# Four pairs of PSUM banks for large and small tiles, adjacent keys in the window attention, spread bias products and a new weighting in the planner

## The chip, the cores and the metric

The kernel runs on one core of one Trainium2 chip. The core has a TensorE (PE in the profile; PEld is its loading of the stationary operand), a VectorE (DVE), a ScalarE (ACT), a GpSimd (POOL) and a SyncE (SP), which here only issues DMAs. The engines run side by side, each through its own queue in order, and wait for each other through semaphores. Matrix products land in PSUM, from where DVE or ACT take them into SBUF. The metric is the device time of one execution in microseconds (us). The three runs of the kernel before took 1317.29, 1317.72 and 1319.53 us, so the median is 1317.72 us.

## The reference, cut to what matters

The input is `x` of shape (4, 512, 128), float32. Six stages follow, each added to `x`:

```
x = x + 0.5 * rwkv_ffn(layernorm(x))          # three 128x128 products, relu^2, sigmoid
x = x + attention(layernorm(x))               # 16 heads of 64, 512 keys, relative bias
x = x + 0.5 * rwkv_ffn(layernorm(x))
x = x + 0.5 * local(layernorm(x))             # two layers
x = x + min_gru(layernorm(x))                 # a scan over time
x = x + 0.5 * local(layernorm(x))             # two layers
```

One layer of `local` is what the change touches most. With 8 heads of 64 and a window of 64:

```
h = shift_token(x)
q, k, v = split(h @ wqkv)                     # then l2norm, scales and rotary factors on q and k
bk, bv  = the window before and the own window of k and v      # 128 keys for each 64 queries
sim  = q @ bk.T, masked to  i - 64 <= j <= i
x    = x + softmax(sim) @ bv @ wo
h    = layernorm(shift_token(x)) * lg + lb
a, g = split(h @ w1 + b1)                     # 341 columns each
x    = x + (a * gelu(g)) @ w2 + b2
```

## The kernel before, in words

Everything is kept in SBUF, with the 128 features on the partitions and 512 times of one sequence along a row (`xTs[b]`). There are four sequences b; a sequence has NT = 4 blocks t of 128 times.

**A planner orders the work.** The kernel's code doesn't issue instructions. A `Recorder` for each engine writes operations down with a cost in us, a virtual due time `vt` and the tiles that they touch; `plan.bundle(cost, mode)` makes one operation of several PE products. `Plan.plan` then simulates the engines and picks at each step the operation that can start first, the one with the least due time among those that can start together. It looks `HORIZON` us of due time ahead. A PE bundle whose `mode` (full, row or col) differs from the last one's is counted `MODE_BIAS` later, an ACT function that needs another table `TABLE_BIAS` later. `Plan.emit` issues what was picked, engine by engine in that order, and `pin` fixes it. So the order within an engine, and the buffers, are decided by this plan before the kernel runs, and the chip waits where the real durations differ. `STEP`, `TURN`, `ATTN`, `LATE` (lines 49 and 50) set the due times: a query block of the attention is due every `STEP`, a step of a local layer every `TURN`.

**Modes.** In `full` mode a product uses the whole 128x128 array. `row` mode takes halves of the contraction (64 rows each, two heads at once): the scores of the attention (64*128, one bundle is two products of 512 columns) and of the window attention (64*64). `col` mode takes halves of the output columns: the weighted sums over the values (128*64).

**Buffers.** `Memory` (lines 344 to 399) gives tiles out by kind. In SBUF 33 buffers serve either one `pair` tile or two `half` tiles each. In PSUM there are two tiles of kind A (`psA`, two banks each, 1024 columns) and four of kind S (`psS`, one bank each, 512 columns).

**Attention** (`unit`, lines 545 to 627). For each of 8 pairs of heads and 4 sequences, four query blocks q: a bundle of scores into an A tile; two DVE operations that add the bias and find the maximum (`tensor_tensor_reduce`, line 587); two exponentials on ACT; a multiplication on POOL; later eight transposes into two S tiles, copied out by DVE (j = 0) and ACT (j = 1); after two q, a col bundle `po` (line 616).

**Local layer** (`local_layer`, lines 637 to 830). Nine kinds of work run as a pipeline over t, listed in `order` and `behind` (lines 792 to 794): `rotate`, `values`, `turn`, `soften`, `turn_back`, `weigh`, `turn_outputs`, `project`. `turn` transposes q and k into `qTs[t]` and `kTs[t]`, two halves. `soften` makes the scores of the two 64-query windows of block t. For the lower window (PSUM partitions 0 to 63) the own 64 keys are in `kTs[t]`, the 64 before them in `kTs[t - 1]` (zeros at t = 0), so there are two products of 64 columns for each head; for the upper window one of 128 columns. That is 24 products in a bundle, 64 such bundles. `turn_back` puts the values of the lower window together in `vm` by two DMAs, own keys on partitions 0 to 63 and earlier ones on 64 to 127.

**Bias products** (lines 945 to 957). `lb @ w1` of each layer, six products of one column in one S tile for each layer (12 in all), each followed by a DVE addition out of the same tile. All are due near the end of the attention.

Of the kernel before, what the change touches and what calls it, by code (L numbers as in the profile page):

```python
# [9 lines left out]
ALU = mybir.AluOpType  # L10
# [4 lines left out]
P = 128  # L15
B, T, D = 4, 512, 128
NT = T // P
# [28 lines left out]


PAIRS = 33
STEP, TURN = 3.6, 11.7
ATTN, LATE, LAG = 25.0, 410.0, 4  # L50

class Tile:

# [61 lines left out]
class Plan:  # L115
# [1 line left out]

    LATENCY, HORIZON, SWITCH, TABLE = 0.07, 36.0, 0.1, 1.28  # L120
    MODE_BIAS, TABLE_BIAS = 2.0, 11.3

    def __init__(self, tc, memory):
        self.tc, self.nc, self.memory = tc, tc.nc, memory
# [45 lines left out]
    def plan(self):  # L170
# [13 lines left out]
        free, mode, order, wire = {}, "full", [], 0.0  # L184
        unplanned = sorted(self.ops, key=lambda o: -o.vt)
        table = None
        while unplanned:
            while unplanned and unplanned[-1].start is not None:
                unplanned.pop()
# [76 lines left out]
    def emit(self, order):  # L266
        table = None
        for op in order:
            since = len(self.nc.cur_bb.bb.instructions)
            if op.table and op.table != table:  # L270
                table = op.table
                self.nc.scalar.add_instruction(  # L272
                    mybir.InstLoadActFuncSet(
                        name=self.nc.get_next_instruction_name(),
                        engine=mybir.EngineType.Activation, act_func_set_id=table,
                    )
                )
            for call in op.calls:
                call()
            self.pin(since)  # L280
# [63 lines left out]
class Memory:  # L344


    def __init__(self, slots, pairs):
        self.slots = slots
        self.pairs = pairs
        self.free = {k: [0.0] * len(s) for k, s in slots.items()}  # L350
        self.halves = [[0.0, 0.0] for _ in pairs]

    def when(self, kind):
        inf = float("inf")
        if kind == "half":
            return min((f for h in self.halves for f in h if f is not None), default=inf)
        if kind == "pair":
            return min((max(h) for h in self.halves if None not in h), default=inf)
        return min((f for f in self.free[kind] if f is not None), default=inf)

    def take(self, t):
        if t.kind == "half":
            at = [
                (f, h[1 - j] is not None, i, j)
                for i, h in enumerate(self.halves) for j, f in enumerate(h) if f is not None
            ]
            first = min(a[0] for a in at)
            _, _, i, j = min((a for a in at if a[0] <= max(first, self.now)), key=lambda a: a[1:])
            self.halves[i][j], t.slot, base = None, (i, j), self.pairs[i][:, j * HALF : (j + 1) * HALF]
        elif t.kind == "pair":  # L370
            at = [(max(h), -i) for i, h in enumerate(self.halves) if None not in h]
            first = min(a[0] for a in at)
            i = -min((a for a in at if a[0] <= max(first, self.now)), key=lambda a: a[1])[1]
            self.halves[i], t.slot, base = [None, None], (i, None), self.pairs[i]
        else:
# [3 lines left out]
        if t.kind == "va":  # L379
            t.real = base  # L380
            return
        n = 1
        for d in t.shape[1:]:
            n *= d
        v = base[: t.shape[0], :n]
        if len(t.shape) > 2:
            names = "abc"[: len(t.shape) - 1]
            v = v.rearrange(
                f"p ({' '.join(names)}) -> p {' '.join(names)}", **dict(zip(names, t.shape[1:]))
            )  # L390
        t.real = v

    def give(self, t):
        if t.kind == "half":
            self.halves[t.slot[0]][t.slot[1]] = t.end
        elif t.kind == "pair":
            self.halves[t.slot[0]] = [t.end, t.end]
        else:
            self.free[t.kind][t.slot] = t.end


HALF = T + 8
# [3 lines left out]
def tile_macaron(ctx: ExitStack, tc: tile.TileContext, i: dict, out: bass.AP):  # L406
# [6 lines left out]
    def real(name, shape, pool=pool):  # L413
# [36 lines left out]
    pool_.memset(tiny[:, 1:2], 1e-24)  # L450
    ones_sb = const("ones", [P, P])
    pool_.memset(ones_sb, 1.0 / D)
    zeros_sb = const("zeros", [P, WIN])
    pool_.memset(zeros_sb, 0.0)

    def vec(col, n=P):
        return vecs[:n, col : col + 1]
# [179 lines left out]
    def local_layer(l, h):  # L637
# [47 lines left out]
        def turn(t):  # L685

            u = us.pop(t)
            qTs[t] = plan.tile("half", [P, H1 // 2, P])
            kTs[t] = plan.tile("half", [P, H1 // 2, P])
            for g, dst in enumerate((qTs[t], kTs[t])):  # L690
                ptp = plan.tile("S", [P, H1 // 2, P])
                with plan.bundle(0.44):
                    for pr in range(H1 // 2):
                        c = g * INNER + pr * P
                        pe.transpose(ptp[:, pr, :], u[:, c : c + P], ident)
                act.copy(dst, ptp)

        def soften(t):


            qT, kT = qTs.pop(t), kTs[t]
# [26 lines left out]
        def turn_back(t):  # L728


            vm = vms[t] = plan.tile("half", [P, H1, DX])
            dma.dma_start(out=vm[0:64], in_=vas[t][0:64])
            if t == 0:
                pool_.memset(vm[64:128], 0.0)
# [189 lines left out]
    for l in range(DEPTH):  # L924
# [17 lines left out]
            pool_.tensor_tensor(tab[l], tab[l], sc, ALU.mult)  # L942
            tab[l] = tab[l].rearrange("p n (g d) -> p n g d", d=DH)

        pb = plan.tile("S", [P, 2, NHC])
        for g in range(2):
            for c in range(NHC):
                n = min(P, HID - c * P)
                c0 = g * HID + c * P
                pe.matmul(  # L950
                    pb[:n, g, c : c + 1], lhsT=w1_sb[l][:, c0 : c0 + n], rhs=vec(V_LNB + l),
                    start=True, stop=True,
                )
                v0 = (V_B1G if g else V_B1A) + l * NHC + c
                dve.tensor_tensor(
                    b1_sb[:n, l, g, c : c + 1], pb[:n, g, c : c + 1], vec(v0, n), ALU.add
                )
# [21 lines left out]
def _constants():  # L979
# [12 lines left out]


    p, c = np.arange(P)[:, None], np.arange(KEYS)[None, :]
    upper = p < WIN
    at = np.where(upper, (c + WIN) % KEYS, c)
    seen = (at >= p % WIN) & (at <= p % WIN + WIN)
    mask = np.stack([seen & ~(upper & (at < WIN)), seen], axis=1)
    mask = np.where(mask, f4(0.0), f4(NEG)).astype(f4)

    half = np.arange(0, DH, 2, dtype=f4)
# [73 lines left out]
```

## Time and profile before

| what | value |
| --- | --- |
| runs of the kernel before | 1317.29, 1317.72, 1319.53 us (median 1317.72) |
| the profiled execution, its own time | 1317.3 us |
| its span in the trace, first to last instruction | 1315.5 us |
| granted TensorE clock, mean over the span | 0.992 |
| DVE, ACT, POOL busy | 970.1, 893.1, 741.4 us |
| PE products in the trace | 10892 |
| ACT table loads, each 1283 ns | 76 |

The span is 1.8 us shorter than the profiled execution's time: what lies around it is outside the trace. The work runs through the stages one after another with some overlap at their borders. Up to about 50 us come the loads and the first `rwkv`, to about 480 us the attention, to about 600 us the second `rwkv` and the first steps of the local layers, to about 880 us the first local stage, to about 1000 us the recurrence and the passage into the second local stage, and from there on the second local stage.

A float32 product that is no transpose appears as two records in the trace (6614 products make 10892 records, 2336 of them transposes with one record each). Records of PE overlap, and their ends are modelled. What a bundle costs PE is therefore read as the distance from its start to the start of the next bundle.

### The profile page before, as it was taken

The numbers are of one execution on the slowest core, as the hardware profiler recorded it, in microseconds if no ns is written. First come the engines' busy times: TensorE is split into PE (matmuls) and PEld (weight loads), VectorE is DVE, ScalarE is ACT, GpSimd is POOL, SyncE is SP. The second block draws the span as 40 slices with busy tenths as digits, with TensorE's granted clock in tenths as the row PEclk, the third lists the DMA queues.
The fourth block names the chain that finished last, engine by engine and source line by source line (L and its number), as shares of the span: only waits on it lengthen the run. The fifth ranks groups of instructions, "written<-read, shape, count | busy, mean of one in ns | idle before, by whom it ended". The sixth has DMA issues, their size and how long they took to land. (4 is left out here: it accounts for less than half of the span.)

```text
span 1315.5 us, 27611 instructions
## 1 busy us (share of the span) xinstructions
PE 1265.9 (96%) x10892; PEld 791.5 (60%) x10892; DVE 970.1 (74%) x1875; ACT 893.1 (68%) x1698; POOL 741.4 (56%) x445
## 2 busy tenths in 40 slices
PE   7999999999999999899999999999889999999997
PEld 3455566556565655457766666664355766666673
DVE  4766666667677657888887787876888887787774
ACT  5866666656666646767777767777577777777774
POOL 3645455554554736768856655623578766665620
PEclk9999999999999989999999999999899999999999
DMA  4775000000000000010101100000110101100000
GB/s 114 224 223 175 0 1 1 1 1 1 1 2 0 1 0 17 13 26 22 31 22 22 26 22 22 22 1 1 29 26 22 30 17 27 26 22 22 14 18 24
DMA packets 26773, 41.79 MB, mean 32 GB/s; under 512 B 3386, under 2 KB 14180, under 8 KB 26644
## 3 DMA queue, kind: packets, MB, share of 16 engines
q1 hardware_dynamic: 26356, 39.95, 11.2%
q8 instruction: 86, 1.41, 0.5%
q14 instruction: 43, 0.35, 0.1%
q10 hardware_dynamic: 288, 0.08, 0.0%
HBM read 23.99 MB, written 9.49 MB: 25 GB/s over the span
## 5 line engine op out<-in xcount | busy, mean ns | idle before, releaser
L302 POOL TENSOR_TENSOR pair<-pair,small 128x1024 f32<-128x1024 f32 x256 | 485.5, 1902 | 319.7 <-DVE small L302 281.0
L302 PEld LDWEIGHTS psS<-ident,pair 128*128 128x128 f32 x2320 | 266.4, 142 | 155.3 <-issue 122.1
L302 POOL TENSOR_TENSOR pair<-pair,pair 128x1024 f32<-128x1024 f32 (+2 forms) x111 | 213.7, 1929 | 218.7 <-DVE pair L302 112.2
L302 ACT COPY pair<-psS 128x512 f32<-128x512 f32 x484 | 264.5, 591 | 86.1 <-PE psS L302 68.4
L302 PE MATMUL psS<-ident,pair 128*128 128x128 f32 x2320 | 310.0, 277 | 11.7 <-DVE pair L302 5.0
L302 PE MATMUL psS<-pair,pair 128*64 128x65 f32 (+3 forms) x2352 | 263.9, 310 | 1.0 <-DVE pair L302 1.0
L302 ACT ACTIVATE pair<-pair,small 128x512 f32<-128x512 f32 x256 | 182.8, 717 | 120.2 <-DVE small L302 119.9
L302 PEld LDWEIGHTS psS<-pair,pair 128*64 128x64 f32 (+1 forms) x2352 | 172.3, 144 | 68.7 <-issue 16.9
L302 DVE CUSTOM_DVE_ANT_0 pair<-psA,pair 128x512 f32<-128x512 f32 x256 | 167.0, 684 | 44.5 <-PE psA L302 44.5
L302 DVE COPY pair<-psS 128x512 f32<-128x512 f32 (+1 forms) x192 | 114.7, 599 | 69.4 <-PE psS L302 61.6
L302 DVE TENSOR_REDUCE small<-pair 128x8 f32<-128x1024 f32 (+1 forms) x128 | 151.8, 1211 | 0.8
L302 PE MATMUL psA<-pair 64*128 64x512 f32 (+3 forms) x728 | 142.7, 513 | 0.6 <-DVE pair L302 0.6
L302 ACT ACTIVATE pair<-pair 128x512 f32<-128x512 f32 (+1 forms) x152 | 122.2, 810 | 30.8 <-DVE pair L302 13.5
L302 PE MATMUL psA<-pair,pair 64*64 64x64 f32 (+2 forms) x2728 | 134.1, 263 | 1.8 <-DVE pair L302 1.8
L302 PE MATMUL psA<-wqkv,pair 128*128 128x512 f32 x256 | 123.7, 606 | 2.8 <-DVE pair L302 2.8
L302 DVE TENSOR_TENSOR pair<-psA,sin 128x512 f32<-128x512 f32 x128 | 87.5, 684 | 39.4 <-ACT pair L302 29.3
L302 ACT ACTIVATE pair<-psA 128x1024 f32<-128x1024 f32 x64 | 65.7, 1026 | 65.3 <-PE psA L302 52.8
L302 PEld LDWEIGHTS psA<-pair,pair 64*64 64x64 f32 (+1 forms) x2728 | 84.9, 135 | 30.7 <-issue 22.8
L272 ACT ACT_TABLE_LOAD x75 | 96.2, 1283 | 1.3
L302 PE MATMUL psA<-pair,w 128*128 128x512 f32 (+1 forms) x192 | 89.3, 598 | 4.1 <-DVE pair L302 2.8
L302 DVE TENSOR_TENSOR pair<-psA,mask 128x1024 f32<-128x1024 f32 x64 | 78.0, 1219 | 11.2 <-PE psA L302 5.6
L302 PEld LDWEIGHTS psA<-pair 64*128 64x128 f32 (+2 forms) x728 | 52.5, 170 | 55.4 <-issue 44.9
(81 smaller groups left out, 1454.1 us busy)
## 6 DMA issues: line engine op xcount, KB each, us to landing
pair<-va SPq DMA_DIRECT2D x112, 130.0 KB, 2.3
table<-tdram SPq DMA_DIRECT2D x16, 511.5 KB, 7.0
pair<-table SPq DMA_DIRECT2D x16, 448.0 KB, 4.0
wqkv<-in_L_ffn_wqkv_dram SPq DMA_DIRECT2D x2, 768.0 KB, 8.1
pair<-in_x_dram SPq DMA_DIRECT2D x4, 256.0 KB, 3.5
out_dram<-pair SPq DMA_DIRECT2D x4, 256.0 KB, 2.3
w<-in_L_ffn_w_dram SPq DMA_DIRECT2D x2, 341.0 KB, 5.9
pair<-in_L_attn_wq_dram SPq DMA_DIRECT2D x8, 64.0 KB, 5.3
```

The source lines that it names most:

```text
L272: self.nc.scalar.add_instruction(mybir.InstLoadActFuncSet(name=self.nc.get_next_instruction_name(), engine=mybir.EngineType.Activation, ac ...
L302: real(*[a.resolve() if isinstance(a, View) else a for a in args], **{k: a.resolve() if isinstance(a, View) else a for k, a in kw.items()},)
```

## The change: what it does

1. **PSUM**: the two A and four S tiles become four pairs of banks, `banks0` to `banks3`. An A tile takes a whole pair, an S tile one bank of a pair; the rule by which they are given out is that of the SBUF pairs and halves.
2. **Adjacent keys**: `kTs[t]` becomes a pair tile of 64 + 128 columns, with the last 64 keys of the block before ahead of its own. A DMA copies those 64 columns out of `kTs[t]` into `kTs[t + 1]`; at t = 0 POOL clears them. `soften` then has, for each head and each window, one product of 128 columns: 16 in a bundle. The mask, and the two halves of `vm`, follow the new order of the keys.
3. **Bias products**: the six of a layer become three bundles of two products, in S tiles of their own and with due times spread over the attention.
4. **Planner**: `MODE_BIAS` from 2.0 to 10.2, `TABLE_BIAS` from 11.3 to 17.0, `HORIZON` from 36.0 to 27.4, `TURN` from 11.7 to 11.1, `ATTN` from 25.0 to 20.5. A PE operation that follows a pause is counted dearer (`IDLE`, `COLD`). The first ACT operation loads table set 6 ahead of itself (`FIRST`); before, the first two ACT operations came with a load each.

```diff
-STEP, TURN = 3.6, 11.7
-ATTN, LATE, LAG = 25.0, 410.0, 4
+STEP, TURN = 3.6, 11.1
+ATTN, LATE, LAG = 20.5, 410.0, 4
...
-    LATENCY, HORIZON, SWITCH, TABLE = 0.07, 36.0, 0.1, 1.28
-    MODE_BIAS, TABLE_BIAS = 2.0, 11.3
+    LATENCY, HORIZON, SWITCH, TABLE = 0.07, 27.4, 0.1, 1.28
+    IDLE, COLD, FIRST = 2.5, 8.0, 6
+    MODE_BIAS, TABLE_BIAS = 10.2, 17.0
...
-            if op.engine == "tensor" and op.mode != mode:
-                cost, mode = cost + self.SWITCH, op.mode
+            if op.engine == "tensor":
+                if op.mode != mode:
+                    cost, mode = cost + self.SWITCH, op.mode
+
+                if at - free.get("tensor", -self.IDLE) >= self.IDLE:
+                    cold = at + self.COLD
+                cost += min(cost, max(0.0, cold - at) / 2)
...
-            if op.table and op.table != table:
-                table = op.table
+            need = op.table or (self.FIRST if op.engine == "scalar" and not op.bytes and table is None else table)
+            if need != table:
+                table = need
                 self.nc.scalar.add_instruction(
...
     memory = Memory(
         {
-            "A": [real(f"psA{n}", [P, 2 * T], psum) for n in range(2)],
-            "S": [real(f"psS{n}", [P, T], psum) for n in range(4)],
...
-        [real(f"pair{n}", [P, 2 * HALF]) for n in range(PAIRS)],
+        {
+            ("half", "pair"): [real(f"pair{n}", [P, 2 * HALF]) for n in range(PAIRS)],
+            ("S", "A"): [real(f"banks{n}", [P, 2 * T], psum) for n in range(4)],
+        },
     )
...
             qTs[t] = plan.tile("half", [P, H1 // 2, P])
-            kTs[t] = plan.tile("half", [P, H1 // 2, P])
-            for g, dst in enumerate((qTs[t], kTs[t])):
+
+            if t == 0:
+                kTs[t] = plan.tile("pair", [P, H1 // 2, WIN + P])
+                pool_.memset(kTs[t][:, :, :WIN], 0.0)
+            for g, dst in enumerate((qTs[t], kTs[t][:, :, WIN:])):
...
+            if t + 1 < NT:
+                kTs[t + 1] = plan.tile("pair", [P, H1 // 2, WIN + P])
+                dma.dma_start(out=kTs[t + 1][:, :, :WIN], in_=kTs[t][:, :, P:])
...
-            with plan.bundle(1.02, "row"):
+            with plan.bundle(0.9, "row"):
                 for pr in range(H1 // 2):
                     for j in range(2):
                         hp = slice(j * DH, (j + 1) * DH)
-                        before = kTs[t - 1][hp, pr, WIN:] if t else zeros_sb[hp, :]
-                        for c, keys in enumerate((kT[hp, pr, :WIN], before)):
+                        for blk in range(2):
+                            c = slice(blk * WIN, (blk + 1) * WIN)
                             pe.matmul(
-                                sc[:WIN, j, pr, c * WIN : (c + 1) * WIN], lhsT=qT[hp, pr, :WIN],
-                                rhs=keys, start=True, stop=True,
+                                sc[c, j, pr, :], lhsT=qT[hp, pr, c],
+                                rhs=kT[hp, pr, blk * WIN : blk * WIN + KEYS], start=True, stop=True,
                             )
-                        pe.matmul(
-                            sc[WIN:, j, pr, :], lhsT=qT[hp, pr, WIN:], rhs=kT[hp, pr, :],
-                            start=True, stop=True,
-                        )
...
-            dma.dma_start(out=vm[0:64], in_=vas[t][0:64])
+            dma.dma_start(out=vm[64:128], in_=vas[t][0:64])
...
-                dma.dma_start(out=vm[64:128], in_=vas[t - 1][64:128])
+                dma.dma_start(out=vm[0:64], in_=vas[t - 1][64:128])
...
-        pb = plan.tile("S", [P, 2, NHC])
-        for g in range(2):
-            for c in range(NHC):
...
+        now = plan.vt
+        for c in range(NHC):
+            n = min(P, HID - c * P)
+            plan.vt = ATTN + (l * NHC + c + 2) * B * NT * STEP
+            pb = plan.tile("S", [P, 2])
+            with plan.bundle(0.3):
+                for g in range(2):
+                    c0 = g * HID + c * P
+                    pe.matmul(
+                        pb[:n, g : g + 1], lhsT=w1_sb[l][:, c0 : c0 + n], rhs=vec(V_LNB + l),
+                        start=True, stop=True,
+                    )
...
+        plan.vt = now
```

More of the change, by code (lines that the diff above doesn't have):

```diff
@@ L183, in plan @@
                 ready.setdefault(op.engine, []).append((0.0, op))
-        free, mode, order, wire = {}, "full", [], 0.0
+        free, mode, order, wire, cold = {}, "full", [], 0.0, 0.0
         unplanned = sorted(self.ops, key=lambda o: -o.vt)
-        table = None
+        table = self.FIRST
         while unplanned:
@@ L344, with __init__ @@
 class Memory:
-    def __init__(self, slots, pairs):
+    def __init__(self, slots, paired):
         self.slots = slots
-        self.pairs = pairs
         self.free = {k: [0.0] * len(s) for k, s in slots.items()}
-        self.halves = [[0.0, 0.0] for _ in pairs]
+        self.paired, self.now = {}, 0.0
+        for (small, large), pairs in paired.items():
+            halves = [[0.0, 0.0] for _ in pairs]
+            self.paired[small] = pairs, halves, False
+            self.paired[large] = pairs, halves, True
     def when(self, kind):
         inf = float("inf")
[L355 to L359, printed above, removed]
-    def take(self, t):
[L362 to L375, printed above, removed]
+        if kind not in self.paired:
+            return min((f for f in self.free[kind] if f is not None), default=inf)
+        _, halves, large = self.paired[kind]
+        if large:
+            return min((max(h) for h in halves if None not in h), default=inf)
+        return min((f for h in halves for f in h if f is not None), default=inf)
+    def take(self, t):
+        if t.kind not in self.paired:
             f = self.free[t.kind]
@@ L378, in take @@
             f[i], t.slot, base = None, i, self.slots[t.kind][i]
-        if t.kind == "va":
-            t.real = base
-            return
+            if list(base.shape) == list(t.shape):
+                t.real = base
+                return
+        else:
+            pairs, halves, large = self.paired[t.kind]
+            if large:
+                at = [(max(h), -i) for i, h in enumerate(halves) if None not in h]
+                first = max(min(at)[0], self.now)
+                i = -min((a for a in at if a[0] <= first), key=lambda a: a[1])[1]
+                halves[i], t.slot, base = [None, None], (i, None), pairs[i]
+            else:
+                at = [
+                    (f, h[1 - j] is not None, i, j)
+                    for i, h in enumerate(halves) for j, f in enumerate(h) if f is not None
+                ]
+                first = max(min(at)[0], self.now)
+                _, _, i, j = min((a for a in at if a[0] <= first), key=lambda a: a[1:])
+                n = pairs[i].shape[1] // 2
+                halves[i][j], t.slot, base = None, (i, j), pairs[i][:, j * n : (j + 1) * n]
         n = 1
@@ L393, in give @@
     def give(self, t):
[L394 to L398, printed above, removed]
+        if t.kind not in self.paired:
             self.free[t.kind][t.slot] = t.end
+            return
+        i, j = t.slot
+        for k in (0, 1) if j is None else (j,):
+            self.paired[t.kind][1][i][k] = t.end
 HALF = T + 8
@@ L452, in tile_macaron @@
     pool_.memset(ones_sb, 1.0 / D)
-    zeros_sb = const("zeros", [P, WIN])
-    pool_.memset(zeros_sb, 0.0)
     def vec(col, n=P):
@@ L695, in turn @@
                         pe.transpose(ptp[:, pr, :], u[:, c : c + P], ident)
-                act.copy(dst, ptp)
+                act.copy(dst, ptp, n=T)
+            if t + 1 < NT:
+                kTs[t + 1] = plan.tile("pair", [P, H1 // 2, WIN + P])
+                dma.dma_start(out=kTs[t + 1][:, :, :WIN], in_=kTs[t][:, :, P:])
         def soften(t):
-            qT, kT = qTs.pop(t), kTs[t]
+            qT, kT = qTs.pop(t), kTs.pop(t)
             sc = plan.tile("A", [P, 2, H1 // 2, KEYS])
-            with plan.bundle(1.02, "row"):
+            with plan.bundle(0.9, "row"):
                 for pr in range(H1 // 2):
@@ L731, in turn_back @@
             vm = vms[t] = plan.tile("half", [P, H1, DX])
-            dma.dma_start(out=vm[0:64], in_=vas[t][0:64])
+            dma.dma_start(out=vm[64:128], in_=vas[t][0:64])
             if t == 0:
-                pool_.memset(vm[64:128], 0.0)
+                pool_.memset(vm[0:64], 0.0)
             else:
-                dma.dma_start(out=vm[64:128], in_=vas[t - 1][64:128])
+                dma.dma_start(out=vm[0:64], in_=vas[t - 1][64:128])
             e = es.pop(t)
@@ L943, in tile_macaron @@
             tab[l] = tab[l].rearrange("p n (g d) -> p n g d", d=DH)
-        pb = plan.tile("S", [P, 2, NHC])
-        for g in range(2):
-            for c in range(NHC):
[L948 to L953, printed above, removed]
+        now = plan.vt
[10 more added lines that the diff above has]
+                    )
+            for g in range(2):
                 v0 = (V_B1G if g else V_B1A) + l * NHC + c
                 dve.tensor_tensor(
-                    b1_sb[:n, l, g, c : c + 1], pb[:n, g, c : c + 1], vec(v0, n), ALU.add
+                    b1_sb[:n, l, g, c : c + 1], pb[:n, g : g + 1], vec(v0, n), ALU.add
                 )
+        plan.vt = now
         dve.tensor_scalar(w1_sb[l], w1_sb[l], vec(V_LNG + l), None, ALU.mult)
@@ L994, in _constants @@
     p, c = np.arange(P)[:, None], np.arange(KEYS)[None, :]
[L995 to L998, printed above, removed]
+    seen = (c >= p % WIN) & (c <= p % WIN + WIN)
+    mask = np.stack([seen & ~((p < WIN) & (c < WIN)), seen], axis=1)
     mask = np.where(mask, f4(0.0), f4(NEG)).astype(f4)
```

## The prediction

> **What bounds the kernel now.** I read the page's busy shares first, then its slices, then the same by stretches, then PE's timeline.
>
> ```profile
> span 1315.5 us, 27611 instructions
> ...
> PE 1265.9 (96%) x10892; PEld 791.5 (60%) x10892; DVE 970.1 (74%) x1875; ACT 893.1 (68%) x1698; POOL 741.4 (56%) x445
> ...
> PE   7999999999999999899999999999889999999997
> ```
>
> ```profile
> 50.00:450.00 400.00, 399.32 (x2484) 236.51 (x2486) 271.96 (x747) 249.62 (x592) 208.44 (x123) 1.00 0.14 42
> 450.00:600.00 150.00, 143.43 (x960) 80.86 (x956) 112.55 (x213) 97.33 (x196) 94.97 (x62) 0.98 0.06 13
> ...
> 800.00:1000.00 200.00, 182.76 (x1644) 110.79 (x1643) 157.96 (x223) 140.72 (x231) 108.30 (x66) 0.97 0.07 16
> 1000.00:1250.00 250.00, 247.09 (x2849) 171.29 (x2847) 200.95 (x319) 186.88 (x319) 162.31 (x88) 1.00 0.10 23
> ```
>
> The columns are: stretch, its length, busy us of PE, PEld, DVE, ACT and POOL, granted clock, DMA. PE is full in the attention and in the local stages (247.1 of 250 us), where no other engine is above 80%. It idles at the start, at 450 to 600 and at 800 to 1000. As PE's ends are modelled, I checked this on the starts of its bundles: adding up the usual distance from start to start for each kind of bundle gives 1219 us, and all distances together 1307. So 88 us are waits, of which 14 lie before 50 us, 17 at 450 to 600 and 32 at 750 to 1000. The rest of the time is PE's own work, and what the change takes from that work counts in full unless waits grow.
>
> **Changes of form.** PE's timeline shows what they cost (start, length, operation):
>
> ```profile
> 304.20 0.60 PE L302 MATMUL psS<-ident,pair 128*128 128x128 f32 x4
> 304.64 1.88 PE L302 MATMUL psA<-pair,pair 128*128 128x512 f32 x4
> 306.36 1.04 PE L302 MATMUL psS<-ident,pair 128*128 128x128 f32 x8
> 307.32 1.95 PE L302 MATMUL psS<-pair,pair 128*64 128x256 f32 x16
> 309.20 1.99 PE L302 MATMUL psA<-pair 64*128 64x512 f32 x8
> 311.12 0.66 PE L302 MATMUL psS<-ident,pair 128*128 128x128 f32 x4
> ```
>
> Four transposes ahead of another full bundle take 0.44 (304.20 to 304.64). Eight ahead of a col bundle take 0.96, not 0.88: leaving full costs some 0.09. A `po` bundle takes 1.88 ahead of scores (307.32 to 309.20), and 1.75 in the three places where another of its form follows: leaving col costs 0.12, and 0.075 for the narrower bundles of `weigh` (0.57 against about 0.5). Two score bundles take 1.92, and each of them 0.96, whether the second or a transpose follows: leaving row costs no more than staying in it.
>
> In the instruction order of the changed kernel, changes between full, row and col fall from 415 to 238: from full 154 to 88, from col 123 to 76 (61 to 37 of them after `po`), from row 138 to 74. The Trainium skill (TensorEngine Tiling, Key Properties) says that changing the tiling mode drains TensorE, which would make every one of the 177 worth 0.10, **17.7 us**. By the rows it is 66 x 0.095 + 24 x 0.12 + 23 x 0.075 = **10.9 us**, since the row bundles pay their tenth anyway. The row decides. 6 of these 10.9 us lie in the attention (two changes fewer in each of the 32 units), the rest in the local layers; all are on PE, which sets the end there.
>
> **The window scores.** 24 products become 16.
>
> ```profile
> 1093.41 1.24 PE L302 MATMUL psA<-pair,pair 64*64 64x64 f32 x48
> 1094.59 1.98 PE L302 MATMUL psA<-wqkv,pair 128*128 128x512 f32 x4
> ```
>
> A bundle takes 1.18 us. No row shows the new form. In both kernels each quarter of the array streams the same columns (64 + 64 before, 128 after, for four pairs of heads), so only what the dispatch loses can be won. The nearest row for eight records of 128 columns in sequence is `wo`'s four products (0.89 us from start to start). With the 0.10 of a row bundle's end this makes 0.99 at best, a gain of 0.19; the other end is 1.18, no gain. A loss I exclude: fewer records over the same columns. I take 1.03, near the row: 0.15 x 64 = **9.6 us** (0 to 12).
>
> **The bias products.**
>
> ```profile
> 479.52 0.88 PE L302 MATMUL psS<-vecs,w 128*128 128x1 f32 x8
> 480.64 0.38 PE L302 MATMUL psS<-vecs,w 128*128 128x1 f32 x2 [0.25 <-DVE b L302]
> 481.34 1.36 PE L302 MATMUL psS<-vecs,w 128*85 128x1 f32 x12 [0.31 <-DVE b L302]
> 483.08 0.45 PE L302 MATMUL psS<-vecs,w 128*85 128x1 f32 x2 [0.39 <-DVE b L302]
> 483.39 3.76 PE L302 MATMUL psA<-pair,pair 128*128 128x512 f32 x4
> ```
>
> 12 of them take 3.87 us (479.52 to 483.39), since each waits for DVE's addition out of the same tile. Bundled by two they take about 12 x 0.15: **2.1 us** less.
>
> **The first table.** ACT's first load stands behind a wait:
>
> ```profile
> 9.00 1.28 ACT L302 ACT_TABLE_LOAD   x1 [9.00 <-DVE pair L302]
> 10.30 0.63 ACT L302 ACTIVATE pair<-pair 128x512 f32<-128x512 f32 x1
> 10.94 1.28 ACT L272 ACT_TABLE_LOAD   x1
> ```
>
> PE waits at 10.98 for that square. With the load issued ahead of the wait, **1.3 us** go; the second load lay beside a product anyway. Of the other loads 14 go as well (76 to 61 in all), 18 us of ACT. ACT is not late in the full stretches, so I count nothing; at most 4 us in 800 to 1000.
>
> **What it adds.** (a) 48 DMAs of adjacent keys on SP's queue. The nearest row, `pair<-va` of the same 130 KB, lands in 2.3 us. In the new order at least 8.3 us of PE work lie between the last thing SP waits for and the scores; the DMAs of `vm` behind them on SP have at least 14.5. Nothing; without that cover, 48 x 2.3. (b) Sixteen clears on POOL, which idles 44%: nothing. (c) Banks are reused sooner. Before, 7 banks are written again within 0.5 us of PE work and lost 5.9 us, 39 between 0.5 and 0.95, which lost 2.3. After, 6 and 86: 5.1 + 5.2, so **2.1 us** more. (d) The tail: the mean and variance products of the last sequence now follow each other, where a `w1` pair (1.7 us) lay between some of them. I take **2 us**. The look-ahead of 27.4 instead of 36 is shown by no row: between -15 and +20 us of waits (half of what 750 to 1000 has, or two thirds more); I take 0, as the stages' order is the same.
>
> **Sum**: -10.9 - 9.6 - 2.1 - 1.3 + 2.1 + 2.0 = -19.8. Against the profiled execution's own time, 1317.3 (span 1315.5), this makes 1297.5; that execution lay 0.4 under the median of the runs, so **1298**.
>
> **The case against: bursts.** The new order has all four score bundles of a unit in a row. The skill (TensorEngine Tiling, PSUM Bottleneck) warns that tiling speeds up TensorE but not the evacuation of PSUM. DVE needs per bundle 2 x (0.684 + 0.083) = 1.53 us by its rows (the operation and its accumulator read), PE 0.96. By the rule alone a burst of four is 6.1 us of DVE against 3.84 of PE. By the order it need not wait: the first three bundles have pairs of their own, the fourth takes the first's, 1.92 us after that is complete, when DVE has had its 1.53; and the copies of transposes stand between DVE's reads of the second and third bundle, not behind the fourth.
>
> **Rivals.**
> - *The burst holds PE*: if DVE runs late and the transposes behind the burst wait for it, PE loses 6.1 - 3.84 less the 0.49 + 0.86 of the two bundles that need no copied bank, about 0.9 us in each of 32 units: 1298 + 29 = **1327**. It decides from 0.6 us a unit. For it: the cover is 0.4 us. Against: DVE is busy 68% of the attention, and the copies' place. Chance 0.10.
> - *Waits shrink too*: banks that serve either kind, fewer loads on ACT, a plan that counts a cold PE. Of the 63 us of waits at the start, 450 to 600 and 750 to 1000, 25 go: **1273**. For it: at 800 to 1000 PE waits for ACT and DVE. Against: those waits are chains of one sequence that the change leaves. Chance 0.24.
> - *Less comes through*: the new window scores gain nothing and the middle waits grow by 5: 1298 + 9.6 + 5 = **1313**. Chance 0.16, a fifth of it within the limit of no change.
> - *The forecast*, 1289 to 1307: chance 0.50.
>
> The range 1274 to 1314 takes in the forecast, the third, and most of the second. Under 0.2% (2.6 us), about what a measurement of this kernel tells, is no change: 0.03. Slower 0.11, faster 0.86.
>
> **What would show it.** Scores of the window at about 1.03 from start to start; a transpose to transpose step still 0.44; in the attention about 14.4 us for a unit instead of 14.6; the bias products in pairs without DVE between; PE's waits near 90 us in all, with 750 to 1000 no worse. If a unit of the attention takes over 15 us with PE waiting for DVE behind the scores, the burst is right; if PE's idle time in the passage doubles, the look-ahead is.

## The result and the profile after

The changed kernel takes **1424.65 us** (median of 6 runs, 1420.19 to 1427.74) where the kernel before takes 1317.26 us (6 runs, 1315.27 to 1319.53): a ratio of **1.0816**, 95% interval 1.0792 to 1.0839. It is 107 us slower; 20 us less were forecast. The profiled execution has a span of 1425.9 us at a mean granted clock of 0.988.

The page of the changed kernel, its shares and PE's 40 slices:

```profile
span 1425.9 us, 25648 instructions
...
PE 1277.0 (90%) x9868; PEld 777.0 (54%) x9868; DVE 944.8 (66%) x1875; ACT 879.1 (62%) x1683; POOL 742.6 (52%) x460
...
PE   6899998999999998988999999998888999999985
```

There are 1024 product records fewer, as the new window scores should give. But every engine's share is lower than before, PE's included: no engine is loaded more, and each waits more. The same by stretches (stretch, length, busy us of PE, PEld, DVE, ACT, POOL, granted clock, DMA):

```profile
50.00:450.00 400.00, 369.87 (x2285) 219.36 (x2285) 246.83 (x701) 232.87 (x552) 190.13 (x103) 1.00 0.14 43
...
1000.00:1250.00 250.00, 221.65 (x2011) 137.59 (x2009) 189.68 (x277) 169.57 (x293) 164.06 (x97) 0.99 0.13 29
```

PE was full in both (399.3 and 247.1 us) and now lacks 30 and 28 us at a clock of 1.00 and 0.99 (1.00 before). By the accounting of the prediction (the usual distance from start to start of each kind of bundle, summed, is PE's own work; the rest is waits) own work fell from 1219 to 1182 us and waits rose from 88 to 235. So the loss is in the waits, and they are spread evenly: 5.6 to 7.3 us in every 50 us from 100 to 450, where before had 0.4 to 1.1.

One unit of the attention on PE's timeline shows two such waits (start, length, operation, and in brackets the idle time before it and what ended it):

```profile
305.44 3.67 PE L309 MATMUL banks<-pair,pair 128*64 128x256 f32 x32
309.04 3.80 PE L309 MATMUL banks<-pair 64*128 64x512 f32 x16
312.77 0.66 PE L309 MATMUL banks<-ident,pair 128*128 128x128 f32 x4
313.26 1.02 PE L309 MATMUL banks<-pair,pair 128*128 128x512 f32 x2
315.07 0.66 PE L309 MATMUL banks<-ident,pair 128*128 128x128 f32 x4 [0.79 <-DVE pair L309]
...
317.13 1.09 PE L309 MATMUL banks<-ident,pair 128*128 128x128 f32 x8 [0.67 <-DVE xT L309]
```

The first line is two `po` bundles, the second the burst of four score bundles. DVE's timeline of the same stretch:

```profile
309.18 0.76 DVE L309 COPY pair<-banks 128x256 f32<-128x256 f32 x2 [2.81 <-PE banks L309]
...
314.32 0.69 DVE L309 COPY pair<-banks 128x512 f32<-128x512 f32 x1 [1.50 <-PE banks L309]
...
316.38 0.69 DVE L309 TENSOR_TENSOR xT<-banks,xT 128x512 f32<-128x512 f32 x1 [0.76 <-ACT pair L309]
```

To read it one needs to know which bank each tile got; the built program tells. The two `po` bundles lie in the two banks of `banks2`. The second one starts at 307.21, so the first is ready by then. DVE is idle, and yet the copy of the first begins at 309.18, just after the **second** is complete (305.44 + 3.67 = 309.11). Four us later the same: transposes in the first bank of `banks0` are complete near 313.4 (312.77 + 0.66), `wo`'s product goes to the second bank, and the copy of the transposes (314.32) begins when that product is through (313.26 + 1.02). PE's next transposes want the first bank again, and so PE stands still until 315.07. At 317.13 it is the other way round: PE writes one bank of `banks0` when DVE is done with reading the other (316.38 + 0.69). A copy or a product waits for work that it shares no byte and no bank with.

### The profile page after: what moved, and what is told of

It reads as the page before. It is cut to its first block, busy times and chain, and to the rows that moved or that the text cites. A ratio compares the mean times of both kernels' runs of the same rounds, so it can differ in the third digit from the quotient of the medians.

```text
span 1425.9 us, 25648 instructions
## 1 busy us (share of the span) xinstructions
PE 1277.0 (90%) x9868; PEld 777.0 (54%) x9868; DVE 944.8 (66%) x1875; ACT 879.1 (62%) x1683; POOL 742.6 (52%) x460
## 5 line engine op out<-in xcount | busy, mean ns | idle before, releaser
L309 ACT COPY pair<-banks 128x512 f32<-128x512 f32 (+1 forms) x518 | 286.9, 587 | 192.1 <-PE banks L309 154.6
L309 PE MATMUL banks<-pair,pair 64*64 64x128 f32 (+4 forms) x4520 | 375.5, 301 | 12.9 <-ACT pair L309 6.0
L309 PE MATMUL banks<-ident,pair 128*128 128x128 f32 x2320 | 318.8, 278 | 70.7 <-DVE pair L309 26.6
L309 PEld LDWEIGHTS banks<-ident,pair 128*128 128x128 f32 x2320 | 259.9, 142 | 209.2 <-issue 93.6
L309 PEld LDWEIGHTS banks<-pair,pair 64*64 64x64 f32 (+2 forms) x4520 | 248.8, 140 | 103.4 <-issue 33.3
L309 DVE COPY pair<-banks 128x512 f32<-128x512 f32 (+1 forms) x224 | 132.6, 610 | 163.4 <-PE banks L309 138.5
L309 PE MATMUL banks<-wqkv,pair 128*128 128x512 f32 x384 | 189.5, 613 | 16.5 <-ACT pair L309 6.8
L309 DVE CUSTOM_DVE_ANT_0 pair<-banks,pair 128x512 f32<-128x512 f32 x256 | 166.7, 683 | 13.8 <-PE banks L309 12.8
L309 ACT ACTIVATE pair<-pair 128x512 f32<-128x512 f32 (+1 forms) x152 | 121.4, 810 | 55.2 <-DVE pair L309 31.5
L309 DVE TENSOR_REDUCE small<-pair 128x16 f32<-128x1024 f32 (+1 forms) x128 | 153.4, 1212 | 1.4
L309 PE MATMUL banks<-pair,w 128*128 128x512 f32 (+2 forms) x288 | 134.3, 611 | 4.2 <-POOL pair L309 2.5
L309 DVE TENSOR_TENSOR pair<-banks,cos 128x1024 f32<-128x1024 f32 x64 | 77.8, 1216 | 11.5 <-ACT pair L309 11.1
L309 DVE TENSOR_TENSOR pair<-banks,mask 128x1024 f32<-128x1024 f32 x64 | 78.0, 1219 | 11.1 <-PE banks L309 9.3
```

Of the source, the lines that this page charges most:

```text
L309: real(*[a.resolve() if isinstance(a, View) else a for a in args], **{k: a.resolve() if isinstance(a, View) else a for k, a in kw.items()},)
```

## The experiments

**Theory 1, tied banks.** Two tiles cut from one declared PSUM tile wait for each other. A reader of one half waits for the product in the other half, if that was issued ahead of it; a product into one half waits for the readers of the other. **Theory 2, the pool.** Serving both kinds out of the same banks, in the new order with its bursts, makes banks come free late and PE wait.

Three things were counted. In the built program: how many waits between engines name an instruction that works on the same declared PSUM tile but on no byte in common ("tied"). In the trace: how many readers of one half begin only when the neighbour's product ends though their own was complete ("held"), and for how long in all; both counts depend a little on how a bundle and a short delay are taken, so they are good for comparing kernels and not to the last one. And PE's own work and waits, as above.

| kernel | time, us | ratio to before (interval) | tied | held (us) | own work / waits |
| --- | --- | --- | --- | --- | --- |
| before | 1317.3 | | 131 | 26 (22) | 1219 / 88 |
| after | 1424.65 | 1.0816 (1.0792 to 1.0839) | 818 | 248 (249) | 1182 / 235 |
| e1: after, banks apart | 1303.6 | 0.9904 (0.9877 to 0.9931) | 137 | 5 (4) | 1196 / 97 |
| e2: before, banks tied | 1451.25 | 1.1015 (1.0996 to 1.1034) | 991 | 280 (237) | 1220 / 219 |
| e3: after, old numbers | 1433.1 (one run) | | 834 | 332 (278) | 1213 / 210 |
| e4: before, new numbers | 1321.9 (one run) | | 131 | 5 (3) | 1204 / 107 |
| e5: eight banks | **1281.2** | 0.9728 (0.9710 to 0.9746) | 21 | 0 | 1178 / 92 |
| e6: banks apart, old numbers | 1303.3 | 0.9892 (0.9877 to 0.9906) | 127 | 26 (23) | 1209 / 83 |
| e7: before, one pair tied | 1397.6 | 1.0609 (1.0593 to 1.0624) | 575 | 159 (144) | 1219 / 168 |
| e8: eight banks, old numbers | 1292.65 | 0.9813 (0.9799 to 0.9828) | 10 | 0 | 1200 / 82 |
| e9: large tiles split, no pool | 1302.6 | 0.9893 (0.9877 to 0.9910) | 19 | 0 | 1188 / 104 |
| e10: eight banks, old keys | 1288.9 | 0.9789 (0.9775 to 0.9804) | 21 | 0 | 1184 / 94 |
| e11: eight banks, look-ahead 36 | 1281.5 | 0.9737 (0.9720 to 0.9753) | 18 | 0 | 1178 / 92 |
| e12: eight banks, fewer forms | 1293.65 | 0.9821 (0.9802 to 0.9841) | 23 | 0 | 1173 / 108 |

**e1. Everything of the change but the pairs of banks.**

```diff
+            "A": [real(f"psA{n}", [P, 2 * T], psum) for n in range(2)],
+            "S": [real(f"psS{n}", [P, T], psum) for n in range(4)],
...
-            ("S", "A"): [real(f"banks{n}", [P, 2 * T], psum) for n in range(4)],
```

> The changed kernel with PSUM as it was before (two A tiles of two banks, four S tiles of one bank, each a tile of its own), all else changed, and planned anew. Theory 1 (tied banks: two S tiles that are halves of one declared tile wait for each other's products and readers): PE's own work stays at some 1195 to 1205 us by the distances of starts, its waits fall from 235 to about 90, the time to about 1290 us (1275 to 1305). Theory 2 (the planner's new numbers bunch the work, and DVE and ACT can't take the bunches out of PSUM): still above 1380 us.

Measured 1303.6 us. The waits are back at 97. The loss sits in the pairs of banks; whether in the tie or in the pool, this run can't tell, since both went.

**e2. The kernel before with nothing but the tie.** The order of instructions on every engine is the same as before.

```diff
+    two = [real(f"psS{n}", [P, 2 * T], psum) for n in range(2)]
...
-            "S": [real(f"psS{n}", [P, T], psum) for n in range(4)],
+            "S": [t[:, k * T : (k + 1) * T] for t in two for k in range(2)],
```

> The kernel before with one edit: its four S tiles are declared as the halves of two tiles of two banks. The plan and the order of instructions on every engine are the same as before. Theory 1: DVE and ACT hold back copies until the neighbour's product is done, PE waits for readers of the neighbour; the time rises to about 1390 us (1350 to 1430). Theory 2: nothing depends on the declaration, 1317 us.

Measured 1451.25 us: 134 us for a change of two lines, in which no instruction, no size and no place in the order differs. (The banks are numbered anew: the small tiles lie in banks 0 to 3 instead of 4 to 7, the large ones the other way round. PE's own work shows nothing of it, 1220 us for 1219.) More than expected, and theory 2 can't give it, since there is no pool. The same instructions of PE and DVE in the two kernels, first before, then e2:

```profile
296.75 1.02 PE L302 MATMUL psS<-pair,pair 128*128 128x512 f32 x2
297.62 1.47 PE L302 MATMUL psS<-ident,pair 128*128 128x128 f32 x12
...
296.96 0.69 DVE L302 COPY pair<-psS 128x512 f32<-128x512 f32 x1
```

```profile
321.46 1.02 PE L302 MATMUL psS<-pair,pair 128*128 128x512 f32 x2
322.32 1.04 PE L302 MATMUL psS<-ident,pair 128*128 128x128 f32 x8
323.87 0.65 PE L302 MATMUL psS<-ident,pair 128*128 128x128 f32 x4 [0.51 <-DVE xT L302]
...
322.52 0.69 DVE L302 COPY pair<-psS 128x512 f32<-128x512 f32 x1 [0.99 <-PE psS L302]
```

The first line is `wo`'s product, the copy takes the transposes out of the bank beside it. Before, the copy runs while the product does (296.96); in e2 it begins when the product is through (321.46 + 1.02 = 322.48). The last four of the twelve transposes go to the bank that the copy left at 323.21, but begin only after DVE is done with `wo`'s result in the other half (323.81). PE's waits in e2 (engine and line, what it waited for: us in all, times, longest):

```profile
PE psS L302 <- ACT pair L302: 50.6, 79, 3.0
PE psS L302 <- DVE pair L302: 49.2, 66, 3.2
```

In the kernel before, these two waits are 5.2 us (11 times) and 13.4 us (15 times).

**e3 and e4. The planner's numbers, each way round.** e3 is the changed kernel with the old numbers and without the cold cost, e4 the kernel before with the new ones.

```diff
-STEP, TURN = 3.6, 11.1
-ATTN, LATE, LAG = 20.5, 410.0, 4
+STEP, TURN = 3.6, 11.7
+ATTN, LATE, LAG = 25.0, 410.0, 4
...
-    LATENCY, HORIZON, SWITCH, TABLE = 0.07, 27.4, 0.1, 1.28
+    LATENCY, HORIZON, SWITCH, TABLE = 0.07, 36.0, 0.1, 1.28
...
-    MODE_BIAS, TABLE_BIAS = 10.2, 17.0
+    MODE_BIAS, TABLE_BIAS = 2.0, 11.3
...
-                cost += min(cost, max(0.0, cold - at) / 2)
```

> The changed kernel with the planner's numbers of before (HORIZON 36, MODE_BIAS 2, TABLE_BIAS 11.3, TURN 11.7, ATTN 25, no cold PE), the four pairs of banks kept. Theory 1: still slow, above 1380 us. Theory 2: about 1305 us, since the bunches are gone.

> The kernel before with the planner's new numbers and nothing else; PSUM, keys and bias products as before. Theory 1: 1300 to 1320 us, some 5 us of changes of form less. Theory 2: near 1420 us.

Measured 1433.1 and 1321.9 us. The numbers aren't the loss. Without the pool they are no gain either: in e4 PE's own work is 15 us less than before, and its waits 19 us more.

**e5. The pool without the tie.** Eight tiles of one bank; a large tile is any two of them, and the operations that spanned both (the square and the products in `rotate`, the mask's addition in `soften`) are split in two.

```diff
+            "S": [real(f"bank{n}", [P, T], psum) for n in range(8)],
...
-            ("S", "A"): [real(f"banks{n}", [P, 2 * T], psum) for n in range(4)],
...
-                sc = plan.tile("A", [P, 2, T])
+                sc = [plan.tile("S", [P, T]) for _ in range(2)]
...
-            dve.tensor_tensor(e, sc.rearrange("p j r k -> p (j r) k"), mask, ALU.add)
+            for j in range(2):
+                dve.tensor_tensor(e[:, j * (H1 // 2) : (j + 1) * (H1 // 2), :], sc[j], mask, ALU.add)
```

> The changed kernel with the pool of banks kept but no tile of PSUM wider than one bank: eight tiles of one bank, a large tile takes any two of them. Rotate's square and products and the mask's addition, which spanned both banks, are split in two (about +0.9 us of DVE and ACT for each of 32 blocks). Theory 1 (halves of one declared tile hold each other): no product or reader names a neighbour any more, PE's waits fall from 235 us to about 90, time about 1290 us (1270 to 1310), at or below the 1303.6 of the kernel with large and small banks apart. Theory 2 (serving both kinds out of one pool brings bursts and late banks): stays above 1380 us.

Measured **1281.2 us**: 36 us faster than before, 143 us faster than the change, and still a pool with bursts. The split does cost DVE time (977 us busy, 945 in the changed kernel), and yet the pool is the fastest kernel so far. Theory 2 falls here. PE's timeline of the same unit, and under it DVE's:

```profile
307.19 3.67 PE L312 MATMUL bank<-pair,pair 128*64 128x256 f32 x32
310.80 3.70 PE L312 MATMUL bank<-pair 64*128 64x512 f32 x16
314.43 0.66 PE L312 MATMUL bank<-ident,pair 128*128 128x128 f32 x4
314.92 1.02 PE L312 MATMUL bank<-pair,pair 128*128 128x512 f32 x2
315.78 1.91 PE L312 MATMUL bank<-ident,pair 128*128 128x128 f32 x16
...
321.55 3.67 PE L312 MATMUL bank<-pair,pair 128*64 128x256 f32 x32
```

```profile
309.19 0.42 DVE L312 COPY pair<-bank 128x256 f32<-128x256 f32 x1 [1.16 <-PE bank L312]
310.91 0.42 DVE L312 COPY pair<-bank 128x256 f32<-128x256 f32 x1 [1.30 <-PE bank L312]
```

The first `po` is copied at 309.19, while PE fills the bank of the second, and no bracket stands behind a PE line. A unit takes 14.36 us from `po` to `po` (307.19 to 321.55), with the tie 16.71 (305.44 to 322.15). The Trainium skill (PSUM — Partial Sum Buffer, PSUM bank collisions raise a hardware error) asks that PSUM be guarded by bank and group of 32 partitions. The 21 waits that are left in e5 name work on other columns of the same bank, none in another bank; the tie guards by declared tile, here two banks.

PE's waits in this kernel, the first two rows; in the changed kernel they are 55.2 us (74 times) and 50.6 us (78 times):

```profile
PE bank L312 <- ACT pair L312: 14.6, 23, 2.1
PE bank L312 <- DVE pair L312: 14.4, 15, 3.6
```

**e6. Banks apart and the old numbers**: of the change only the adjacent keys, the spread bias products and the first table are left.

> Two large and four small tiles of their own and the planner's old numbers, so of the change only the adjacent keys, the spread bias products and the first table are left. Theory 1: no ties; own work of PE about 14 us more than with the new numbers (1196 + 14), waits some 10 to 20 us less (97 down to about 80): 1300 us (1292 to 1312), so the new numbers bring nothing. Rival: the new numbers bring the gain of the kernel with banks apart; then this one is at 1317 and not faster than before.

Measured 1303.3 us, the same as e1. As long as large and small tiles have banks of their own, the new numbers bring nothing; these three parts alone make 14 us.

**e7. Half a dose.** The kernel before with two of the four small tiles tied.

```diff
+    two = real("psSS", [P, 2 * T], psum)
...
-            "S": [real(f"psS{n}", [P, T], psum) for n in range(4)],
+            "S": [two[:, :T], two[:, T:]] + [real(f"psS{n}", [P, T], psum) for n in range(2)],
```

> The kernel before with two of the four small tiles as halves of one declared tile of two banks, the other two apart; nothing else, the order on every engine is the same. Theory 1: 103 waits name the neighbour's half, against 188 with both pairs tied and 7 before, so about half of the 134 us: 1317 + 71 = 1388 us (1360 to 1400). Rival (a tile of two banks costs by itself, or the loss comes from something else in that kernel): 1317 or 1451.

Measured 1397.6 us, 80 us over before (expected 71, e2 134). The 103, 188 and 7 of the expectation are a narrower count than the table's: readers that wait for a product in the other half. Divided by the held readers the loss is much the same in three kernels of different build. e7: 80 us for 133 more than before, 0.60 us each. e2: 134 for 254, 0.53 us. The changed kernel against e5: 143 for 248, 0.58 us. This is a quotient, not a measured price: with shorter holds counted too (95 before, 210 in e7, 318 in e2, 294 in the changed kernel, none in e5) it is 0.70, 0.60 and 0.49 us.

The tie also works the other way, on PE directly. PE products that begin only when a reader of the other bank ends, with all else done: 95 in e7 (48 us), 161 in e2 (80 us), 91 in the changed kernel (44 us); one before, none in e1 and e5.

**e8. Eight banks, old numbers.**

> Eight tiles of one bank as a pool, with the planner's old numbers. Theory 1: like the eight banks with the new numbers but 14 us more of PE's own work and some 15 us fewer waits: 1295 us (1275 to 1310). Theory 2 (new numbers need the pool, or the pool delays): above 1380 us.

Measured 1292.65 us. Here the new numbers are worth 11 us (e5), while with banks apart they were worth nothing.

**e9. The large tiles untied, without the pool**: large tiles take two of four banks, small tiles one of the other four.

> The kernel with eight one-bank tiles (1281.2), but without the pool: large tiles take two of four banks of their own, small tiles one of the other four. Against the kernel with two large tiles of two banks and four small ones (1303.6) only the large tiles' halves are untied, so this splits the 22 us between the two. Theory A (the ties inside large tiles cost it: 26 readers were held there for 23 us): 1285 us (1278 to 1291). Theory B (sharing the banks brings it): 1303 us (1298 to 1308). I expect most of it by A.

Measured 1302.6 us: theory A fell, the sharing of banks is what brings the 21 us between here and e5: 10 us of own work and 12 of waits. The expectation stood on the number of another kernel: by the table's count 26 readers were held inside large tiles in e6 (23 us), but in e1, with which e9 is to be compared, only 5 (4 us). With the shared banks the same planner finds an order with 240 changes of form, with banks apart 332.

**e10. Eight banks with the old keys**: the window scores as 24 products again, no copies of keys.

> Eight one-bank tiles with the window scores as 24 products out of two tiles of keys again, no copies of keys to the next block; all else stays. The forecast's term of 9.6 us for the new products: 1281.2 + 9.6 = 1291 us; by the trace of the changed kernel (bundles of 1.03 and 0.92 for 1.18) 12 us: 1293 us. Rival (fewer, wider products gain nothing because each quarter streams as many columns): 1281 us. Range 1287 to 1298.

Measured 1288.9 us: the new products are worth 7.7 us of time here, near the lower end of what was expected; the rival falls.

**e11. Eight banks with a look-ahead of 36.**

> Eight one-bank tiles with the planner's look-ahead of 36 for 27.4 and nothing else. The forecast took no difference (-15 to +20): 1281 us (1275 to 1288). Rival (the shorter look-ahead is what keeps the passage between stages short or makes it long): a change of over 10 us, seen as PE's waits at 800 to 1000.

Measured 1281.5 us: no difference.

**e12. Eight banks, changes of form weighed at 20** instead of 10.2.

> Eight one-bank tiles with the planner's weight of a change of form at 20 for 10.2: in the built order 200 changes of form for 240. If every change costs PE 0.10 us, as the steps from start to start in the traces of the runs show, its own work falls by 4 us: 1277 us (1272 to 1281). Rival (a plan that waits longer for its own form runs the other engines late): waits grow by as much or more, 1281 to 1295 us.

Measured 1293.65 us: a miss. Own work fell as expected (1178 to 1173), but the waits rose from 92 to 108, so the rival holds. PE's first wait in this kernel, against 14.6 us in 23 times above:

```profile
PE bank L312 <- ACT pair L312: 22.9, 41, 2.2
```

e5 and e11 stay the fastest versions found, and beat both kernels.

## Why the prediction was wrong

**The step that failed** is (c) of "What it adds": "Banks are reused sooner", with 2.1 us for it. I had worked out for each bank when it is written again and when its reader is done, bank by bank, as if the two halves of a `banks` tile were as independent as the four `psS` tiles. In the built program they are not: 818 waits name work on the same `banks` tile that touches none of their bytes, nearly all of it in the other bank. This step cost some 121 us (e1 against the changed kernel) to 143 us (e5, which keeps the pool). None of the rivals had it, so the range had no room for it either.

The trace of before had the sign. Its two large tiles already had halves, and their first reader shows the tie. PE's line and DVE's line of that kernel:

```profile
319.50 1.88 PE L302 MATMUL psA<-pair,pair 128*128 128x512 f32 x4
```

```profile
321.48 0.69 DVE L302 COPY pair<-psA 128x512 f32<-128x512 f32 x1 [1.15 <-PE psA L302]
```

The four records are two products, q into one bank and k into the other. q is complete about half way, near 320.5. DVE is idle from 320.33, yet copies q at 321.48, when k is complete (319.50 + 1.88 = 321.38). 26 readers were held so, for 22 us. For the large tiles such ties cost next to nothing: with them untied, e9 takes 1302.6 us where e1 takes 1303.6. The change spread them to every small tile. The halves of `pair` tiles in SBUF, which the kernel before gives out by the same rule, are no precedent. In the changed kernel only 44 waits name a neighbour in a `pair` tile, and those lie between instructions that also share a `banks` tile; no wait there rests on a `pair` tile alone.

**What bounds it** was right: PE, with its own work counting in full unless waits grow. That condition is what broke.

**Changes of form**, 10.9 us, was too small, since a change costs on both of its sides. From product to product, in before and in e5, the last product ahead of a change takes about 0.10 more in every form: 0.20 for 0.11 with a transpose, 0.53 for 0.43 with a score, 0.16 for 0.06 in `weigh`. The first product behind it takes 0.05 to 0.10 more as well: a transpose 0.17 for 0.11, a `po` product 0.27 for 0.22, one of `weigh` 0.11 for 0.06, a score 0.53 for 0.43, a full product of 512 columns 0.96 for 0.86. The rows of bundles, here and in the prediction, show the two together. Two bundles of scores take 1.92 (309.20 to 311.12 before), four take 3.63 in e5 (310.80 to 314.43). The second two thus take 1.71, and entering and leaving row takes 0.21. For `po` it is 1.88 and 3.61 (307.19 to 310.80), so 0.15.

The claim that "leaving row costs no more than staying in it" was wrong. In a pair of score bundles the first pays for entering and the second for leaving, and so both take 0.96. The rule that I weighed against the rows (the Trainium skill, TensorEngine Tiling (Array Packing), Key Properties: changing the tiling mode drains TensorE) was nearer, as every form pays. But priced at 0.10 its 17.7 us were too few too. Outside the window's bundles the changes sum to 60 us before and 34 in e5, 26 us less. With 12.5 for the window's bundles and 2 for the bias products this makes nearly all of the 41 us by which PE's own work fell in e5 (37 in the changed kernel).

**The window scores** were right, 9.6 us forecast. In the changed kernel a bundle that stands alone takes 1.03 (14 of them), as forecast; the two of a pair take 0.92 and 0.98 (25 pairs), where before all 64 stood alone at 1.18. That is 13 us, but part of it is the change of form that is missing inside a pair. e10 has pairs of old bundles too, at 0.98 and 1.12. Against these the new products save 0.14 alone, 0.06 and 0.14 in a pair, 7 us for the 20 single ones and 22 pairs of e5; e10 puts 7.7 us of time on it.

**The bias products**, 2.1 us: the steps that start with one sum to 3.9 us before and 2.0 in e5. Right. **The first table**, 1.3 us: in e6 the load stands at 1.78 instead of 9.00, the first square begins at 9.05 instead of 10.30, and PE's product at 9.73 instead of 10.98, 1.25 us earlier. Right. **The copies of keys**: they landed in 2.3 us, and no PE wait of the changed kernel names them. Right. **The look-ahead**, 0: e11 measures 0.3 us. Right. **The tail**, 2 us, was not measured by itself.

**The burst.** I had written that a unit over 15 us with PE waiting for DVE behind the scores would show the burst right. The sign came (16.71 us), and the burst was not the cause: e5 has the same burst of four and a unit of 14.36 us, against 14.4 forecast. The sign didn't separate the two mechanisms; the question that does is which bank the late reader reads and which product it waits for.

The forecast of 1298 would have been right for e1 within 6 us. For e5 it was too high by 17, mostly the changes of form (26 us for 10.9).

## What to carry to other kernels

Two PSUM tiles that are cut from one declared tile may be tied by the waits of the built program, even where they lie in different banks. When a change alters how buffers are declared, look in the built order at what each wait names, and count those that name work on the same tile but on other bytes; the loss here was 0.5 to 0.7 us for each reader held that way. Declare a PSUM tile for each bank and let a large tile take two, with the operations that span both split: the whole change then brought 36 us instead of losing 107, and 21 of them come from sharing the banks.

Weighing changes of form more pays only while the other engines are not made late. The planner's new numbers together, the weight of 10.2 among them, brought 11 us with shared banks and nothing with banks apart; a weight of 20 instead of 10.2 lost 12.

## What the runs showed of the hardware besides

- A change of form on PE costs 0.15 to 0.20 us in all three forms: about 0.10 on the last product ahead of it, 0.05 to 0.10 on the first one behind it.
- PE begins at half speed, with the granted clock of the first 50 us at 1.00: the first four transposes take 1.08 us in the kernel before and 1.09 in the changed one instead of 0.60, the first products of 512 columns 2.04 and 1.91 instead of 1.02. In the kernel before full speed is there at 19.41 us (four transposes in 0.60), in the changed kernel only at 33.85 us, after some 25 us in which PE pauses 0.8 to 1.5 us at a time. Once it is there, a pause of 1.64 us does not take it away. The first line is the changed kernel's, the second that of the kernel before:

```profile
16.81 2.08 PE L309 MATMUL banks<-pair,ones 128*128 128x512 f32 x2 [1.44 <-ACT pair L309]
```

```profile
24.23 1.12 PE L302 MATMUL psS<-pair,w_k 128*128 128x512 f32 x2 [1.64 <-DVE pair L302]
```

  What brings full speed was not tried. In the changed kernel 24 us of PE's waits lie before 50 us, against 14 before and 9 in e5.
- In the kernel before, at 940.71, two DVE operations of 64x512 with both inputs in SBUF took 2.0 and 3.5 us, where 11 of the other 14 of that kind take 0.66 to 0.73; POOL ran additions and products of two SBUF inputs from 939.81 on. That POOL is the cause was not tried.
